# A 128 + 64 channel convolution and a list schedule with measured durations, in layer 0 of a two-layer network

## The chip, the cores and the metric

The kernel runs on one core of one Trainium2 chip. A core has five engines with a queue of instructions each: TensorE (PE, matrix products, with weight loads shown apart as PEld), VectorE (DVE), ScalarE (ACT), GpSimd (POOL) and SyncE (SP, which here only issues DMAs). The metric is the device time of one execution in microseconds (us). Before the change the median of three runs is 8392.63 us (8389.98 to 8398.43).

## The reference

The input x is [2, 96, 96, 96] (images, channels, rows, columns), and everything is float32 unless a step quantizes. Two layers follow each other. Each adds a mixing block to x and then a small feed-forward block (96 to 384 to 96 channels with rounding to 8-bit and 16-bit floats). Layer 0, which the change is about, does this with d_inner = 192 channels, 16 states and four scan directions k:

```
xz = in_proj_w @ layernorm(x);  xin, z = split(xz)          # 192 + 192 channels
t  = gelu(batchnorm(conv3x3(xin, off1_w) + off1_b))          # 192 -> 192 channels
off = tanh(off2_w @ t) / 95                                  # a shift in y and in x
x_s = bilinear sample of xin at (pixel + off)
x_s -> 512 sequences of 36 tokens, by rows and by columns, forward and backward
dt, B, C = x_proj[k] @ x_s;  delta = softplus(dt_proj[k] @ dt + bias)
h[l] = h[l-1] * exp(delta * A) + (delta * x_s) * B[l]        # 16 states per channel
y[l] = sum over states of h[l] * C[l], + D * x_s
out  = out_proj_w @ (layernorm(sum of the 4 directions) * silu(z))
```

Layer 1 is an attention block with a depthwise 5x5 convolution. The change doesn't touch it.

## The kernel before

**Stripes and units.** Layer 0 is cut into 32 stripes of 6 rows by 96 columns (T = 576 tokens, H2 = 288 half of them). A stripe passes three parts. `_l0_front` normalizes, projects, convolves, samples, and stores delta and delta*x_s to DRAM. `_l0_scan` runs the recurrence. `_l0_back` normalizes y, projects it and runs the feed-forward block. The front of stripe n+1 and the back of stripe n-1 are planned between the scans of stripe n.

The scan of a stripe has 64 units: 2 channel halves h, 2 orders o, 2 directions kk, 4 quarters i of the states, 2 halves c of the tokens. `_l0_section` makes the operations of eight units, in this chain:

- spread (L1056, TensorE): the selection matrix `selb` times B into PSUM `bp`, of which there are two
- product (L1060, DVE): `bp` times delta*x_s (`dur`), 128 x 864
- scan (L1076, DVE): the recurrence along 864 elements into `h`, of which there are six
- times C (L1081, GpSimd): `h` times C (`cre`, four buffers)
- states (L1093, TensorE): the products with `fold` that sum over states into `y`
- decay (L1041, ScalarE), once for two units: exp(A * delta) into `dA`

DMAs bring `dlr` and `dur` (two buffers each, L1026) per section and `cre` (L1036) per quarter.

**The convolution** (`convolve`, L567). The 192 channels lie as two halves of 96 partitions. A result of 96 output channels by 288 tokens is the sum of 18 products: 2 input halves by 9 taps. There are 2 output halves and 2 token halves, so 72 products of 96 x 96 weights, each as two passes (records) in float32. Its weights `w_c1` are loaded first of nearly all in `_l0_weights`. The sampled `x_s` and all the operands of the front lie in two halves of 96, too.

**What sets the order.** Every operation of layer 0 is given to a planner (`_Plan`) with an engine, a cost in us, the tiles that it reads and writes, and a due time. `order` simulates the five engines: it always takes the operation that can start first, where a tie within 0.1 us on one engine is decided by the due time. A result reaches another engine after a `LAG` (0.5 to 1.5 us), the same engine after `SAME` (0.06). A tile needs a free buffer before its first operation can start. `issue` emits the instructions in the planned order, and `_in_order` fixes that order on every engine and on SP. At run time an engine that waits for a semaphore holds everything behind it. Costs come from `_cost` (by columns) and, for the chain, from constants in `_l0_section`. Due times spread over a stripe's 64 tau (tau = 3.4): the front of stripe n is due from 64 n - 90 to 64 n - 12 tau, the back from 64 n + 68 to 64 n + 135, a spread 60 tau before its unit.

The pick in `order`, which the change rewrites, is:

```python
key = (max(at, free[e] + 0.1), worth, o.no)
if pick is None or key < pick[0]:
    pick = (key, at, o)
```

Of the kernel before, what the change touches and what calls it, by code (L numbers as in the profile page):

```python
# [90 lines left out]
class _Op:  # L91
    def __init__(self, eng, cost, run, due, tab):
        self.eng, self.cost, self.run, self.due, self.tab = eng, cost, run, due, tab
        self.deps, self.tiles, self.start, self.end = set(), [], None, None
        self.left, self.then, self.ready = 0, [], 0.0

SAME = 0.06  # L100
LAG = {"pe": 0.5, "dve": 1.5, "act": 0.6, "pool": 1.0, "sp": 1.5}


class _Plan:
# [3 lines left out]
    def __init__(self, k):  # L108
        self.k, self.ops, self.slots, self.queues = k, [], {}, {}
        self.rate = {}  # L110
# [12 lines left out]
    def op(self, eng, cost, run, r=(), w=(), due=0.0, tab=None, also=()):  # L123
        o = _Op(eng, cost * self.rate.get(eng, 1.0), run, due, tab)
        ref = lambda t: t if isinstance(t, tuple) else (t, None)
# [20 lines left out]
    def order(self):  # L146
# [13 lines left out]
        while len(out) < len(self.ops):  # L160
            best = None
            for e, queue in ready.items():
                pick = None
                for o in queue:
                    at = max(free[e], o.ready)
                    for t in o.tiles:
                        if t.slot is None:
                            s = t.place()
                            if s is None:
                                at = None  # L170
                                break
                            at = max(at, s[1] + (SAME if s[2] == e else LAG[e]))
# [6 lines left out]
                    key = (max(at, free[e] + 0.1), worth, o.no)  # L179
                    if pick is None or key < pick[0]:  # L180
                        pick = (key, at, o)
# [21 lines left out]
            for p in o.then:  # L203
                p.left -= 1
                p.ready = max(p.ready, o.end + (SAME if p.eng == o.eng else LAG[p.eng]))
# [77 lines left out]
def _l0_weights(k, a, cp, tmp, ps, dram):  # L283
# [6 lines left out]

    k.w_in = load("in_proj", [C, 4 * C])
    k.w_c1 = load("off1", [C, 2, 9, 2 * C])
# [11 lines left out]
    bnv = tmp.tile([C, 5, 2], F32, tag="bnv", name="bnv")  # L304
    nc.sync.dma_start(bnv, a["bn"])
    k.bn_s = cp.tile([C, 2], F32, tag="bn_s", name="bn_s")
    k.bn_t = cp.tile([C, 2], F32, tag="bn_t", name="bn_t")
    nc.scalar.activation(k.bn_s, bnv[:, 4, :], AF.Sqrt, bias=k.eps5[:C])
    nc.vector.reciprocal(k.bn_s, k.bn_s)
    nc.vector.tensor_tensor(k.bn_s, k.bn_s, bnv[:, 1, :], ALU.mult)  # L310
    nc.vector.tensor_tensor(k.bn_t, bnv[:, 0, :], bnv[:, 3, :], ALU.subtract)
    nc.vector.tensor_tensor(k.bn_t, k.bn_t, k.bn_s, ALU.mult)
    nc.vector.tensor_tensor(k.bn_t, k.bn_t, bnv[:, 2, :], ALU.add)


    off2 = tmp.tile([C, 4], F32, tag="off2", name="off2")
    nc.sync.dma_start(off2, a["off2"])
    k.w_off = cp.tile([C, 4, C], F32, tag="w_off", name="w_off")
    nc.vector.tensor_copy(k.w_off, off2.unsqueeze(2).to_broadcast([C, 4, C]))
# [3 lines left out]
    xp = tmp.tile([C, 2, KG, 6 + 2 * NS], F32, tag="xp", name="xp")  # L323
    nc.sync.dma_start(xp, a["x_proj"])
    k.w_dl = cp.tile([C, 2, 2, C], F32, tag="w_dl", name="w_dl")
# [8 lines left out]
    k.w_bc = cp.tile([C, 2, 2, 4, 2, NS], F32, tag="w_bc", name="w_bc")  # L334
# [94 lines left out]
    ds4 = tmp.tile([C, KG, 2], F32, tag="ds4", name="ds4")  # L429
    nc.scalar.dma_start(ds4, a["Ds"])  # L430
    k.Dsum = cp.tile([C, 2], F32, tag="Dsum", name="Dsum")
    nc.vector.tensor_tensor(k.Dsum, ds4[:, 0], ds4[:, 1], ALU.add)
    nc.vector.tensor_tensor(k.Dsum, k.Dsum, ds4[:, 2], ALU.add)
    nc.vector.tensor_tensor(k.Dsum, k.Dsum, ds4[:, 3], ALU.add)
    k.w_D = cp.tile([C, 2, C], F32, tag="w_D", name="w_D")
    for half in range(2):
        nc.vector.tensor_scalar(
            k.w_D[:, half], k.ident[:C, :C], k.Dsum[:, half : half + 1], None, ALU.mult
# [3 lines left out]
def _cost(eng, cols):  # L442

    if eng == "pe":
        return 0.00175 * cols
    if eng == "act":
        return 0.2 + 0.0009 * cols
    if eng == "pool":
        return 0.2 + 0.00177 * cols
    return 0.08 + 0.00115 * cols  # L450


def _op(S):
    def op(eng, n, run, r, w, also=(), tab=None, times=1):
        S.op(eng, times * _cost(eng, n), run, r, w, also=also, tab=tab)
# [4 lines left out]
def _l0_front(k, P, S, f, x, b, s, at):  # L460
# [13 lines left out]
    def pe(cols, run, r, w, also=()):  # L474
        S.op("pe", _cost("pe", cols), run, r, w, also=also)

    def act(cols, run, r, w, tab=None, times=1):
        S.op("act", times * _cost("act", cols), run, r, w, tab=tab)

    def dve(cols, run, r, w):  # L480
        S.op("dve", _cost("dve", cols), run, r, w)

    def pool(cols, run, r, w):
        S.op("pool", _cost("pool", cols), run, r, w)


    xt, xin = temp([C, 8, HW], "xt"), S.tile(P.front, [C, 2, 8, HW + 4], "xin", 1)
# [39 lines left out]
    def project(half, c):  # L527
        pi = ps("pi")
        pe(N4, lambda: nc.tensor.matmul(
            pi.ap[:C, :N4], k.w_in[:, half * C : (half + 1) * C], xn.ap[:, 4 * c : 4 * c + 4, :],  # L530
            start=True, stop=True), ((xn, c),), (pi,), (xin,))
        act(N4, lambda: nc.scalar.copy(
            xin.ap[:, half, 4 * c : 4 * c + 4, 2 : HW + 2],
            pi.ap[:C, :N4].rearrange("p (r w) -> p r w", w=HW)), (pi,), ((xin, (half, c)),))
# [3 lines left out]
    for half in range(2):  # L538
        for c in range(2):
            project(half, c)  # L540

# [18 lines left out]
    t = temp([C, 2, T], "t")  # L560

    def convolve(oh, c):
        pc = ps("pc")

        def part(ih, tap):
            dy, dx = divmod(tap, 3)
            pe(H2, lambda: nc.tensor.matmul(  # L567
                pc.ap[:C, :H2],
                k.w_c1[:, ih, tap, oh * C : (oh + 1) * C],
                xin.ap[:, ih, 3 * c + dy : 3 * c + dy + 3, dx + 1 : dx + 1 + HW],  # L570
                start=(ih == 0 and tap == 0),
                stop=(ih == 1 and tap == 8),
            ), (xin,), (pc,), (t,))

        for ih in range(2):
            for tap in range(9):
                part(ih, tap)
        act(H2, lambda: nc.scalar.activation(
            t.ap[:, oh, c * H2 : (c + 1) * H2], pc.ap[:C, :H2], AF.Gelu,
            bias=k.bn_t[:, oh : oh + 1], scale=k.bn_s[:, oh : oh + 1]),  # L580
            (pc,), ((t, (oh, c)),), tab="g")

    for oh in range(2):
        for c in range(2):
            convolve(oh, c)
# [3 lines left out]
    fr = temp([C, 2, WIN, HW], "fr", 2)  # L589

    def offset(yx, c):
        po = ps("po")

        def run():
            for half in range(2):
                nc.tensor.matmul(
                    po.ap[:C, :H2], k.w_off[:, 2 * half + yx, :],
                    t.ap[:, half, c * H2 : (c + 1) * H2], start=(half == 0), stop=(half == 1))

        pe(2 * H2, run, ((t, (0, c)), (t, (1, c))), (po,), (fr,))  # L600

        def share():
            v = fr.ap[:, yx, 3 * c : 3 * c + 3].rearrange("p r w -> p (r w)")
            nc.scalar.activation(v, po.ap[:C, :H2], AF.Exp, scale=-2.0)
            nc.scalar.activation(v, v, AF.Ln, bias=k.one[:C])
# [8 lines left out]
    xs0 = f.xs0 = S.tile(P.hand, [C, 2, T], "xs0", 2)  # L614
    xs1 = S.tile(P.front, [C, 2, T], "xs1", 1)
    dif, top, bot = temp([C, 2, 7, HW], "dif"), temp([C, 2, WIN, HW], "top", 1), temp([C, 2, WIN, HW], "bot")
# [3 lines left out]
    def sample(half):  # L620
        v = lambda: xin.ap[:, half, 1:8, 2 : HW + 2]
        fy, fx = lambda: fr.ap[:, 0], lambda: fr.ap[:, 1]
# [1344 lines left out]
```

## Time and profile before

| | |
|---|---|
| median of 3 runs | 8392.63 us |
| profiled execution: its time, its span | 8398.9 us, 8397.1 us |
| mean granted TensorE clock | 0.908 |
| DVE busy | 7812.2 us (93%) |
| scan L1076: count, busy, mean | 2048, 3999.5 us, 1954 ns |
| product L1060 | 2048, 2133.7 us, 1043 ns |
| times C L1081 (GpSimd) | 2048, 3497.2 us, 1714 ns |
| decay L1041 (ScalarE) | 3072, 2156.1 us, 765 ns |
| convolution L567 (TensorE): records, busy, mean | 4608, 1334.6 us, 421 ns |
| states L1093 (TensorE) | 18432, 1847.4 us, 448 ns |
| first scan starts, last scan starts | 144.03 us, 6342.84 us |

The profile is of one execution. An engine is busy while an instruction of it runs. Records overlap: two neighbours on DVE by some 0.08 us, matmuls by much more, so a mean is longer than the spacing from start to start. "Idle before" is the time that an engine stood still ahead of an instruction, with the event that ended it. A wait counts only on the engine that sets the pace of its stage. Layer 0 runs until about 6380 us, where layer 1 loads its input, so the page's shares over the whole span mix two layers.

### The profile page before, as it was taken

The page shows a single profiled execution, that of the slowest core. Times are in us where ns is not written, and L with a number is a line of the kernel's source. Part 1 is how long each engine was busy: PE and PEld are TensorE (multiplying, and loading weights), DVE is VectorE, ACT ScalarE, POOL GpSimd, SP SyncE. Part 2 cuts the span into 40 slices and gives each one's busy share as a digit, 9 for nine tenths or more (in the row PEclk, how much of TensorE's full clock was granted, in tenths as well). Part 3 has the DMA queues.
Part 4 walks back from the last instruction along what each step waited for, and adds up shares of the span by engine and source line. Part 5 has one row for each costly group of instructions (what it writes and reads, how often), then busy time and mean ns, then how long its engine had stood idle before and what let it go on. Part 6 is the DMA issues. An engine that isn't in the chain of part 4 may idle for free. (4 is left out here: it accounts for less than half of the span.)

```text
span 8397.1 us, 118884 instructions
## 1 busy us (share of the span) xinstructions
PE 7293.7 (87%) x43653; PEld 3394.8 (40%) x43653; DVE 7812.2 (93%) x5398; ACT 6318.8 (75%) x10674; POOL 5177.2 (62%) x3835
## 2 busy tenths in 40 slices
PE   7888888888888888888888888888857999989998
PEld 4444444444444444444444444444423223542245
DVE  3999999999999999999999999999996998959988
ACT  5778777777777877777777777777745886778867
POOL 4888888788888888878788888888863000110001
PEclk8899998999889999989999889898857999989999
DMA  3444444444444454444444444444441000110001
GB/s 94 152 155 151 155 152 151 151 152 146 152 149 151 157 159 152 151 150 153 149 152 147 151 151 150 157 150 153 152 131 56 3 2 14 37 47 3 2 22 33
DMA packets 339992, 985.62 MB, mean 117 GB/s; under 512 B 50152, under 2 KB 51872, under 8 KB 339104
## 3 DMA queue, kind: packets, MB, share of 16 engines
q1 hardware_dynamic: 337488, 977.74, 37.0%
q8 instruction: 347, 5.69, 0.3%
q14 instruction: 253, 2.07, 0.1%
q10 hardware_dynamic: 1904, 0.12, 0.0%
HBM read 797.19 MB, written 139.25 MB: 112 GB/s over the span
## 5 line engine op out<-in xcount | busy, mean ns | idle before, releaser
L1081 POOL TENSOR_TENSOR h<-h,cre 128x864 f32<-128x864 f32 x2048 | 3497.2, 1714 | 1130.3 <-DVE h L1076 681.5
L1076 DVE TENSOR_TENSOR_SCAN h<-dA,bp 128x864 f32<-128x864 f32 x2048 | 3999.5, 1954 | 96.1 <-PE y L1093 19.1
L1041 ACT ACTIVATE dA<-dlr,A 128x576 f32<-128x576 f32 x3072 | 2156.1, 765 | 767.2 <-DVE h L1076 678.6
L1060 DVE TENSOR_TENSOR bp<-dur,bp 128x864 f32<-128x864 f32 x2048 | 2133.7, 1043 | 93.3 <-DMA dur<-du_d 39.6
L1093 PE MATMUL y<-h,fold 128*32 128x288 f32 (+2 forms) x18432 | 1847.4, 448 | 318.8 <-POOL h L1081 308.0
L567 PE MATMUL pc<-xin,off 96*96 96x288 f32 x4608 | 1334.6, 421 | 0.0
L1093 PEld LDWEIGHTS y<-h,fold 128*32 128x32 f32 x18432 | 761.3, 118 | 1085.4 <-POOL h L1081 579.9
L1056 PE MATMUL bp<-bt,selb 128*128 128x288 bf16 x2048 | 647.5, 317 | 534.1 <-DVE h L1076 512.7
L1429 ACT ACTIVATE pr<-sc 128x960 f32<-128x960 f32 (+1 forms) x1080 | 953.9, 937 | 200.8 <-PE sc L1425 178.6
L1509 DVE TENSOR_TENSOR sums<-sums,pr 128x3840 f32<-128x3840 f32 (+1 forms) x240 | 959.1, 3996 | 56.2 <-ACT pr L1429 34.2
L567 PEld LDWEIGHTS pc<-xin,off 96*96 96x96 f32 x4608 | 721.9, 167 | 410.2 <-issue 156.4
L1601 POOL MEMSET vch<- 96x32 f32 x16 | 2.4, 153 | 1301.7 <-DVE dist L1463 1208.4
L1056 PEld LDWEIGHTS <-selb 128*128 128x128 bf16 x2048 | 200.6, 98 | 1391.3 <-DVE h L1076 1125.1
L1425 PE MATMUL sc<-qH,kH 32*128 32x480 f32 (+1 forms) x3240 | 627.3, 602 | 10.2 <-DMA q<-qH 5.5
L1425 PE MATMUL sc<-q,kH 32*128 32x480 f32 (+1 forms) x1080 | 564.6, 602 | 0.0
L1491 PE MATMUL av<-pr,vT 128*32 128x480 f32 (+1 forms) x4320 | 533.7, 565 | 3.6 <-ACT av L1516 3.5
L1682 DVE SCALAR_TENSOR_TENSOR acc<-vch,lepe_w,acc 96x1152 f32<-96x1152 f32 x320 | 469.2, 1466 | 8.5 <-ACT vch L1617 0.8
L1425 PEld LDWEIGHTS sc<-qH,kH 32*128 32x128 f32 x3240 | 219.1, 184 | 419.8 <-issue 219.4
L883 POOL TENSOR_TENSOR x<-x,fy 96x576 f32<-96x576 f32 x32 | 55.6, 1738 | 478.7 <-ACT fy L882 414.7
L740 PE MATMUL pt<-xd,w_dt 96*128 96x288 f32 x768 | 299.3, 479 | 24.9 <-ACT r L746 11.9
L759 POOL TENSOR_TENSOR e<-e,du 128x576 f32<-128x576 f32 x192 | 231.1, 1204 | 50.5 <-ACT du L755 49.9
L745 ACT ACTIVATE e<-pt,dt_b 128x288 f32<-128x288 f32 x384 | 190.6, 496 | 93.6 <-PE pt L740 89.2
(270 smaller groups left out, 9858.7 us busy)
## 6 DMA issues: line engine op xcount, KB each, us to landing
cre<-c_d SPq DMA_DIRECT2D x1024, 288.0 KB
dur<-du_d SPq DMA_DIRECT2D x256, 864.0 KB
dlr<-dl_d SPq DMA_DIRECT2D x256, 864.0 KB
x<-xs SPq DMA_DIRECT2D x512, 72.0 KB
du_d<-du SPq DMA_DIRECT2D x128, 288.0 KB
dl_d<-dl SPq DMA_DIRECT2D x128, 288.0 KB
du_d<-du SPq DMA_DIRECT2D x128, 144.0 KB
dl_d<-dl SPq DMA_DIRECT2D x128, 144.0 KB
```

The source lines that it names most:

```text
L567: pe(H2, lambda: nc.tensor.matmul(pc.ap[:C, :H2], k.w_c1[:, ih, tap, oh * C : (oh + 1) * C], xin.ap[:, ih, 3 * c + dy : 3 * c + dy + 3, dx ...
L1041: nc.scalar.activation(dA.ap[:, :, blk, :], dlr.ap[:, blk, :].rearrange("p (c n) -> p c n", c=2), AF.Exp, scale=k.A[:, i, kg, h, blk : blk ...
L1056: nc.tensor.matmul(bp.ap[:, :H2], k.selb[:, kk, i, :], f.bc[o].ap[:, toks], start=True, stop=True)
L1060: nc.vector.tensor_tensor(bp.ap[:, : NBL * H2].rearrange("p (b n) -> p b n", b=NBL)[:, ::-1], dur.ap[:, ::-1, toks], bp.ap[:, :H2].unsquee ...
L1076: nc.vector.tensor_tensor_scan(hv, dv, bv, 0.0, ALU.mult, ALU.add)
L1081: nc.gpsimd.tensor_tensor(ht.ap, ht.ap, cre.ap[:, toks].unsqueeze(1).to_broadcast([128, NBL, H2]), ALU.mult)
L1093: nc.tensor.matmul(dst, k.fold, v, start=False, stop=stop)
L1425: nc.tensor.matmul(two[to // 2][:, to % 2, :n], kH[rows, k0 : k0 + 128], q, start=True, stop=True)
L1429: nc.scalar.activation(pr[:, 2 * i : 2 * i + 2, :n], two[i][:, :, :n], AF.Exp, scale=HD**-0.5)
L1491: nc.tensor.matmul((main if s < HEADS else other)[s * HD : (s + 1) * HD, :n], vT[:, blk, hd, :], pr[:, place(s, p), :n], start=at == 0, st ...
L1509: nc.vector.tensor_tensor(both, both, pr[:, :, :, :n], ALU.add)
L1682: S.op("dve", 1.43, lambda: nc.vector.scalar_tensor_tensor(acc.ap, src(), W.lw[:, t : t + 1], acc.ap, ALU.mult, ALU.add), (vch,), (acc,))
```

## The change

Three things change, all in layer 0.

1. The 192 channels lie as 128 + 64 instead of 96 + 96 in `xin`, `t`, `fr`, `x_s` and their weights. A DMA per stripe copies the 64-channel part of `xin` into partitions 64 to 127, shifted by one column, so that one product takes two taps of it. A result then takes 15 products: nine with the 128 channels ("a"), three with 64 channels and two taps, three with 64 channels and the third tap. The first 128 output channels are convolved for each token half; for the other 64, the two token halves go to partitions 0 to 63 and 64 to 127 of one PSUM tile, as pairs of products.
2. The convolution's weights (`w_ca`, `w_cb`) are loaded by five DMAs of the plan instead of one at the start. Small operands (bn, off2, x_proj, Ds) come in two to four DMAs each.
3. The planner has other costs for layer 0 (`fine`), a shorter lag between operations of the chain (`scan=True`), and a rule for a spread (`first=True`): no operation may be placed on TensorE that would end more than `HOLD` after a spread could start. Layer 1 keeps the old costs and has no such operations.

```diff
 SAME = 0.06
 LAG = {"pe": 0.5, "dve": 1.5, "act": 0.6, "pool": 1.0, "sp": 1.5}
+SCAN_LAG = {"pe": 0.2, "dve": 0.3, "act": 0.2, "pool": 0.2, "sp": 1.5}
+HOLD = 0.15
...
-                            at = max(at, s[1] + (SAME if s[2] == e else LAG[e]))
+                            lag = SCAN_LAG if o.scan else LAG
+                            at = max(at, s[1] + (SAME if s[2] == e else lag[e]))
...
-                    key = (max(at, free[e] + 0.1), worth, o.no)
-                    if pick is None or key < pick[0]:
-                        pick = (key, at, o)
+                    cand.append(((max(at, free[e] + 0.1), worth, o.no), at, o))
+                    if o.first:
+                        hold = at + HOLD if hold is None else min(hold, at + HOLD)
+                for c in cand:
+                    if hold is None or c[2].first or c[1] + c[2].cost <= hold:
+                        if pick is None or c[0] < pick[0]:
+                            pick = c
...
-                p.ready = max(p.ready, o.end + (SAME if p.eng == o.eng else LAG[p.eng]))
+                lag = SCAN_LAG if o.scan and p.scan else LAG
+                p.ready = max(p.ready, o.end + (SAME if p.eng == o.eng else lag[p.eng]))
...
+RATE = {"pe": (0.05, 0.00185), "act": (0.08, 0.00107), "pool": (0.14, 0.0018), "dve": (0.03, 0.00108)}
+LOOSE = {"pe": (0.0, 0.00175), "act": (0.2, 0.0009), "pool": (0.2, 0.00177), "dve": (0.08, 0.00115)}
...
+    S.op("sp", 1.0, lambda: nc.sync.dma_start(
+        xin.ap[64:, 1, :, 1 : HW + 1], xin.ap[:64, 1, :, 2 : HW + 2]),
+        ((xin, (1, 0)), (xin, (1, 1))), ((xin, "on"),))
...
+    terms = [("a", dy, dx) for dy in range(3) for dx in range(3)]
+    terms += [("b", dy, None) for dy in range(3)] + [("b", dy, 2) for dy in range(3)]
...
+    def convolve_rest():
+        pc = ps("pc")
+        for n in range(len(terms)):
+            def run(n=n):
+                for c in range(2):
+                    w, v = term(slice(128, 2 * C), c, n)
+                    nc.tensor.matmul(pc.ap[64 * c : 64 * c + 64, :H2], w, v,
+                                     start=n == 0, stop=n == len(terms) - 1)
+
+            S.op("pe", 0.6, run, reads(n), (pc,), also=(t,))
...
-            S.op("act", 0.76, decay, (dlr,), ((dA, blk),), due=t0 - P.early["act"] * tau, tab="e")
+            S.op("act", 0.69, decay, (dlr,), ((dA, blk),), due=t0 - P.early["act"] * tau, tab="e",
+                 scan=True)
...
-        S.op("pe", 0.3, spread, (f.bc[o],), (bp,), due=t0 - P.early["pe"] * tau)
-        S.op("dve", 1.03, product, (dur,), (bp,), due=t0 - P.early["dve"] * tau)
+        S.op("pe", 0.26, spread, (f.bc[o],), (bp,), due=t0 - P.early["pe"] * tau,
+             scan=True, first=True)
+        S.op("dve", 0.96, product, (dur,), (bp,), due=t0 - P.early["dve"] * tau, scan=True)
...
-        S.op("dve", 2.0, scan, (dA, bp), (ht,), due=t0 + (1.35 - P.early["dve"]) * tau)
+        S.op("dve", 1.87, scan, (dA, bp), (ht,), due=t0 + (1.35 - P.early["dve"]) * tau, scan=True)
...
-        S.op("pool", 1.75, times_c, (cre,), (ht,), due=t0 + (2.3 - P.early["pool"]) * tau)
+        S.op("pool", 1.7, times_c, (cre,), (ht,), due=t0 + (2.3 - P.early["pool"]) * tau, scan=True)
...
-        S.op("pe", 1.0, states, (ht,), (py,), due=t0 + (3.5 - P.early["pe"]) * tau)
+        S.op("pe", 0.84, states, (ht,), (py,), due=t0 + (3.5 - P.early["pe"]) * tau, scan=True)
...
-        S, tau = _Plan(k), 3.4
+        S, tau = _Plan(k, True), 3.4
...
+            S.op("sp", 1.0, lambda dst=dst, src=src: nc.sync.dma_start(dst, src), (), (t,),
+                 due=-88 * tau)
```

The five weight loads carry the due time -88 tau, the first stripe's front starts at -90 tau.

## The prediction

> **What bounds the kernel now.** I read the totals first, then the stages, then the waits of the engine that is full, and last the order of instructions around single waits. The page's totals and slices:
>
> ```profile
> PE 7293.7 (87%) x43653; PEld 3394.8 (40%) x43653; DVE 7812.2 (93%) x5398; ACT 6318.8 (75%) x10674; POOL 5177.2 (62%) x3835
> PE   7888888888888888888888888888857999989998
> DVE  3999999999999999999999999999996998959988
> ```
>
> VectorE is full from the second slice to the thirtieth: that is layer 0. Cut by stage (columns: length, busy us of PE, PE weight loads, DVE, ACT, POOL, then granted clock, DMA share, GB/s):
>
> ```profile
> 0.00:144.00 144.00, 106.48 (x352) 61.60 (x353) 17.95 (x97) 72.14 (x136) 43.10 (x56) 0.87 0.27 80
> 400.00:6000.00 5600.00, 4829.98 (x28645) 2355.49 (x28647) 5470.81 (x3872) 4333.87 (x7511) 4561.38 (x3299) 0.91 0.48 151
> 6345.00:8397.00 2052.00, 1926.13 (x11979) 780.98 (x11976) 1739.93 (x1023) 1540.60 (x2401) 128.71 (x174) 0.95 0.08 21
> ```
>
> So there are three parts: 144 us until the first scan, some 6201 us of scanning, 2052 us of tail and layer 1, which the change doesn't touch. In the middle DVE is busy 5471 of 5600 us, so only idle time can be won there. How much is the floor? An undisturbed stretch of the timeline:
>
> ```profile
> 3002.99 1.04 DVE L1060 TENSOR_TENSOR bp<-dur,bp 128x864 f32<-128x864 f32 x1
> 3004.07 1.95 DVE L1076 TENSOR_TENSOR_SCAN h<-dA,bp 128x864 f32<-128x864 f32 x1
> 3005.94 1.04 DVE L1060 TENSOR_TENSOR bp<-dur,bp 128x864 f32<-128x864 f32 x1
> ```
>
> One unit (product, scan) takes 3005.94 - 3002.99 = 2.95 us. Over two units it is 2.945 (the product after next starts at 3008.88), so 2048 units are about 6031 us; six other DVE instructions a stripe (two each of L928, L524, L843: 0.73, 0.53, 0.43 us less 0.08 of overlap) add 32 x 2.9 = 93. From 144.0 to the end of the last scan at 6344.8 are 6200.8, so some 77 us are idle. The waits of DVE from 144 to 6345 say for whom (total us, times, longest):
>
> ```profile
> DVE bp L1060 <- PE bp L1056: 38.6, 39, 3.3
> DVE h L1076 <- PE y L1093: 19.1, 14, 2.2
> DVE bp L1060 <- POOL h L1081: 9.2, 7, 1.9
> DVE h L1076 <- ACT dA L1041: 5.7, 1, 5.7
> DVE bp L1060 <- PE y L1093: 3.7, 4, 1.7
> ```
>
> With four smaller ones they sum to 80.2. TensorE ends 38.6 + 19.1 + 3.7 = 61.4 of it, though it is not full. Why, one such place of the timeline shows:
>
> ```profile
> 2309.95 2.13 PE L908 MATMUL yva<-ysq,mean 96*96 96x288 f32 x4
> 2312.00 1.18 PE L1093 MATMUL y<-h,fold 128*32 128x288 f32 x6
> 2313.30 1.95 DVE L1076 TENSOR_TENSOR_SCAN h<-dA,bp 128x864 f32<-128x864 f32 x1 [2.20 <-PE y L1093]
> ```
>
> Four `both` operations of the back part run in a row, the fold of h (L1093) that frees the scan's buffer stands behind them, and the scan starts 2.20 us late. Ahead of the scans, the convolution of the first stripe:
>
> ```profile
> 36.48 35.22 PE L567 MATMUL pc<-xin,off 96*96 96x288 f32 x144
> ```
>
> Here nothing hides it: ScalarE, GpSimd and DVE wait, and everything up to the first scan follows in series.
>
> **What the Trainium skill says.** "TensorE: Matmul & The Clock Gate", Part 3, What overlaps: matmuls keep strict order, only weight loads move ahead. The stall above agrees: the fold isn't drawn past 2.13 us of others. "TensorEngine Tiling (Array Packing)", Tiling Modes: 128 x 64 column tiles are two, and different tiles run in parallel; the trace has it for 32-column tiles (three L1093 products of 288 columns take 0.69 us at 3003.85), not for 64. "DMA: Bandwidth & Descriptors", Anatomy of one DMA: about 2 us are fixed; the trace's xt load, issued at 18.09, was used at 23.04, so it does not contradict it.
>
> **The change, part by part.**
>
> *Convolution.* Before: 4 results of 18 products, 72 products in two passes each (144 records), 35.22 / 72 = 0.489 us. After: 15 products per result (nine of 128 input channels, three of 2 x 64 stacked by the shifted copy, three of 64), for two results of 128 output channels, and 15 pairs for the other 64 channels. Rounds: 15 + 15 + 15 = 45, 22.0 us, if the halves of a pair run beside each other; 60, 29.3 us, if not. By the L1093 row I take 45. In the first stripe that saves 13.2 us (bounds 5.9 and 13.2) on the path to the first scan. In the later ones TensorE gets 13.2 of some 194 us back, worth nothing directly, since DVE is the bound; it only thins the blocks. One Gelu fewer (0.59 us) on ScalarE, 77% busy, is hidden by the scans; if ScalarE were the bound it would be 19 us in all.
>
> *Shifted copy.* One more DMA a stripe on SP, 64 x 8 rows of 384 B, 197 KB against 151 GB/s x 194 us = 29 MB. Issue 0.5 us (as other SP rows), landing some 2 us. Behind it on SP stand the loads of cre, dlr, dur. Four cre buffers at 5.9 us a quarter give them about 3 x 5.9 = 17.7 us of lead, so a short wait costs nothing. On TensorE, the nine products that don't need it (4.4 us) hide its landing. I take 0; without that cover 2 us, paid once in the first stripe. The later stripes have slack.
>
> *Setup.* The 1296 KB of weights leave the first load (issued at 1.21; SP's next issue was at 9.89) and come as five DMAs in the plan, most of them before xt. Eleven more small DMAs (bn, off2, xp, Ds in parts) at 0.3 to 0.5 us are about +4.5 us on SP; some have 4-byte runs, and no row shows those. Against it stands a gap of 8.3 us in SP's issues that goes. xt then lands behind about 1 MB, which took 6 to 8 us at the start. I take 0, bounds -6 and +6.
>
> *Operands.* Projection, sampling, x_dbl and D products keep their counts and free sizes; only partitions change. 0.
>
> *The planner.* This is the largest term and no row prices it. The old costs give a unit 1.03 + 2.0 + 0.06 = 3.09 us against 2.945 measured: the plan thinks DVE slower than it is, and puts up to 0.15 us too much between two scans. The new one gives 0.96 + 1.87 + 0.06 = 2.89, now a little short: other engines wait for DVE rather than the reverse. With `first`, nothing may stand on TensorE that would end over 0.15 us after a spread could start; so four pairs in a row can't stand before a waiting spread. Bounds: all 61.4 us of PE waits go; or the order is no better and 0 goes; below that, new waits (a rival). TensorE has room: from a unit of 2.945 the plan takes 0.26 + 0.84 for spread and fold, which leaves 1.85 x 64 = 118 us a stripe for the rest, about 80 at the new costs (convolution 45 x 0.58 = 26, 22 pairs of products at 1.12 = 25, two groups of five at 2.7, single products the rest). I take three quarters, 46 us, since waits for late operands at the head of TensorE's queue remain. Of the 18.8 us of other waits I take 5 (a shorter lag puts times-C and fold nearer to the scan); bounds 0 and 19.
>
> *Sum on the profiled execution* (8398.9 us; span 8397.1 and 1.8 around it): 8398.9 - 13 - 46 - 5 = 8335. The median of the runs, 8392.63, lies 6.3 below the profiled one: **8329 us**, -0.76%. What is late next is DVE itself: 2.945 us a unit.
>
> **Rivals.** *A, only the start is won:* the blocks are replaced by others, TensorE still ends most waits. For it: 39 + 14 waits in 2048 units are rare events, which any new order throws anew; against it: the hold addresses just these. Time 8393 - 13 = 8380 (to 8376 with a few us of waits).
>
> *B, slower: SP's head blocks.* SP issues in order; if the shifted copy stands before its ScalarE copies are done by more than the lead of cre (17.7 us less some 4 to land, so from about 14 us), scans wait for cre through h, 32 times. At 17 us: 3 x 32 = 96, less the 64 won: 8425. For it: SP did sit at xt from 18.83 to 75.67 in the first stripe. Against: the plan knows when the projection ends, the x_s stores wait likewise today, and SP's longest wait for POOL in the middle is 8 us.
>
> *C, better:* every listed wait goes and the setup gains 6: 8393 - 13 - 80 - 6 = 8294.
>
> *D, the pairs don't run side by side:* 8329 + 7 = 8336; inside the forecast, as it only moves the start.
>
> **How the numbers follow.** A measurement here tells about 0.2%, 17 us, from nothing: below 8376 is faster, above 8409 slower. The forecast with D (8300 to 8366): 0.65. C: 0.08. A: 0.14, of which 0.03 lies below 8376. B, or waits for POOL or ACT of that size from the tighter lags: 0.13. Faster 0.65 + 0.08 + 0.03 = 0.76, same 0.11, slower 0.13. The range from 8296 to 8388 holds the forecast, nearly all of A and half of C. It leaves out B and a little of C, under 2 in 10.
>
> **What would show it.** The first scan near 131 instead of 144. The convolution near 22 us in the first stripe, 90 records plus 30 that overlap. DVE's waits for spreads below 10 us and for folds below 8. A unit still 2.945. A stripe of 6200.8 / 32 = 193.8 us falling to about 192.2. If instead DVE waits stand at POOL's h or at dA, the lags are too short for the real engines; if they stand at dur or cre landings, it is B; if the first scan stays at 144, front(1) filled the room or the weights came late.

## The result and the profile after

| | before | after |
|---|---|---|
| median of 20 runs each | 8397.77 us (8389.98 to 8415.25) | 8364.95 us (8346.97 to 8400.17) |
| ratio, 95% interval | | 0.9962 (0.9954 to 0.9969) |
| profiled execution: its time, its span | 8398.9, 8397.1 us | 8360.85, 8359.0 us |
| first scan starts | 144.03 us | 146.78 us |
| first scan to the end of the last ("scan phase") | 6200.8 us | 6159.8 us |
| the rest, layer 1 above all | 2052.3 us | 2052.4 us |

The kernel is 0.38% faster, some 33 us of the 64 that the prediction gave (8392.63 to 8329). The start became 2.8 us longer, the scan phase 41 shorter. The totals and the DVE slices of the page after hardly differ:

```profile
PE 7186.7 (86%) x42885; PEld 3103.1 (37%) x42885; DVE 7626.3 (91%) x5404; ACT 6253.0 (75%) x10610; POOL 5183.8 (62%) x3835
...
DVE  3999999999999999999999999999996998959988
```

DVE is busy 186 us less (7812.2 before) for the same 4096 products and scans. The windows of the kernel after (length, busy us of PE, weight loads, DVE, ACT, POOL, clock, DMA share, GB/s) place that in the middle:

```profile
0.00:147.00 147.00, 113.54 (x335) 57.84 (x336) 18.81 (x104) 72.87 (x136) 43.14 (x56) 0.83 0.29 84
400.00:6000.00 5600.00, 4737.60 (x28056) 2091.56 (x28052) 5318.74 (x3885) 4280.79 (x7465) 4577.24 (x3302) 0.89 0.48 153
6307.00:8359.00 2052.00, 1928.66 (x11982) 781.41 (x11976) 1740.14 (x1023) 1540.72 (x2401) 127.66 (x174) 0.95 0.08 21
```

In the same 5600 us DVE ran 3885 instructions after and 3872 before, in 5319 us of busy time against 5471. So an instruction costs DVE less, and DVE stands still more. Both were unforeseen.

**Why a unit is cheaper.** An undisturbed stretch of DVE's timeline after (start, duration; x2 is two in a row):

```profile
3001.68 2.00 DVE L1112 TENSOR_TENSOR bp<-dur,bp 128x864 f32<-128x864 f32 x2
3003.59 3.79 DVE L1129 TENSOR_TENSOR_SCAN h<-dA,bp 128x864 f32<-128x864 f32 x2
3007.30 2.00 DVE L1112 TENSOR_TENSOR bp<-dur,bp 128x864 f32<-128x864 f32 x2
3009.21 3.79 DVE L1129 TENSOR_TENSOR_SCAN h<-dA,bp 128x864 f32<-128x864 f32 x2
```

DVE no longer alternates. It runs product, product, scan, scan: two units from 3001.68 to 3007.30 are 5.62 us, 2.81 a unit against 2.945 before. All steps from start to start on DVE in the two traces, medians in us (count):

| step | before | after |
|---|---|---|
| product to scan | 1.075 (2015) | 0.961 (1011) |
| product to product | | 0.949 (985) |
| scan to scan | | 1.864 (968) |
| scan to product | 1.871 (1884) | 1.844 (946) |

Before, each scan follows the product that it reads, and starts 1.075 us after it. After, another product or scan stands between, and the step is 0.95 to 0.96. A pair costs 0.949 + 0.961 + 1.864 + 1.844 = 5.618, so 2.809 a unit: 0.136 us less, some 278 us over 2048 units. This is worked out from the medians, as if every unit stood in a pair; 985 of the 1024 possible pairs do. The mean durations hide it, because the records of neighbours overlap: 1936 + 1046 ns after against 1954 + 1043.

**Where it went.** The groups of the page after show the idle time ahead of scan and product (last column, with what ended most of it):

```profile
L1129 DVE TENSOR_TENSOR_SCAN h<-dA,bp 128x864 f32<-128x864 f32 x2048 | 3888.1, 1936 | 145.1 <-PE y L1146 136.1 <-ACT dA L1092 7.1 <-POOL h L1134 1.2
L1112 DVE TENSOR_TENSOR bp<-dur,bp 128x864 f32<-128x864 f32 x2048 | 2063.7, 1046 | 200.5 <-PE bp L1108 65.2 <-DMA dur<-du_d 46.2 <-PE y L1146 43.3
```

In the scan phase the waits of DVE for TensorE are 136.1 + 65.2 + 43.3 = 244.6 us, against 61.4 before. Phase less units less the 93 us of other DVE instructions leaves 6160 - 5753 - 93 = 314 us idle, against 77. So 278 us were won and 237 given back, which is the 41.

The largest single item is unit 38 of the stripe: 103 us in the 31 stripes after the first, as 24 waits in 16 stripes, nearly every second one. Nearly all of it falls where `direct`, described below, stands behind the 40th spread of its stripe in TensorE's order; where it stands ahead of the 39th, DVE waits there at most 0.7 us. So this stall is one of the planned order. One such place in the timeline of all engines:

```profile
2380.73 1.28 ACT L576 ACT_TABLE_LOAD   x1
2382.49 2.24 PE L573 MATMUL pz<-xn,in_proj 96*96 96x288 f32 x4 [2.77 <-ACT zs L576]
2382.62 0.57 ACT L1043 COPY Y<-y 96x504 f32<-96x504 f32 x1
2384.66 1.05 PE L1033 MATMUL y<-xs,w_D 128*32 128x504 f32 x1
2387.80 1.54 PE L1146 MATMUL y<-h,fold 128*32 128x288 f32 x24
2388.54 3.80 DVE L1129 TENSOR_TENSOR_SCAN h<-dA,bp 128x864 f32<-128x864 f32 x2 [8.69 <-PE y L1146]
```

At unit 32 the channel half changes. `y` must be copied out (L1043) and refilled (L1033, `direct`) before the folds of the new half can run. Here both come late, behind the next front's gate on ScalarE (L576, with a table load) and on TensorE (L573). Six units fit into the six `h` buffers, then the scan waits 8.69 us for the folds.

### The profile page after: what moved, and what is told of

Its sections match the earlier page's. It is cut to its first block, busy times and chain, and to the rows that moved or that the text cites. A ratio compares the mean times of both kernels' runs of the same rounds, so it can differ in the third digit from the quotient of the medians.

```text
span 8359.0 us, 117497 instructions
## 1 busy us (share of the span) xinstructions
PE 7186.7 (86%) x42885; PEld 3103.1 (37%) x42885; DVE 7626.3 (91%) x5404; ACT 6253.0 (75%) x10610; POOL 5183.8 (62%) x3835
## 5 line engine op out<-in xcount | busy, mean ns | idle before, releaser
L1129 DVE TENSOR_TENSOR_SCAN h<-dA,bp 128x864 f32<-128x864 f32 x2048 | 3888.1, 1936 | 145.1 <-PE y L1146 136.1
L1112 DVE TENSOR_TENSOR bp<-dur,bp 128x864 f32<-128x864 f32 x2048 | 2063.7, 1046 | 200.5 <-PE bp L1108 65.2
L1146 PE MATMUL y<-h,fold 128*32 128x288 f32 (+2 forms) x18432 | 1824.8, 449 | 87.6 <-POOL h L1134 81.9
L611 PE MATMUL pc<-xin,w_ca 128*128 128x288 f32 x1152 | 370.1, 425 | 0.0
L791 PE MATMUL pt<-xd,w_dt 96*128 96x288 f32 x768 | 319.1, 508 | 10.2 <-ACT r L797 4.9
L812 POOL TENSOR_TENSOR dl<-dl,r 128x576 f32<-128x576 f32 x192 | 231.0, 1203 | 26.4 <-ACT dl L809 16.1
L611 PE MATMUL pc<-xin,w_cb 128*128 128x288 f32 (+1 forms) x768 | 244.5, 429 | 0.0
```

What stands on the lines that cost most here:

```text
L611: nc.tensor.matmul(pc.ap[:, :H2], w, v, start=n == 0, stop=n == len(terms) - 1)
L1112: nc.vector.tensor_tensor(bp.ap[:, : NBL * H2].rearrange("p (b n) -> p b n", b=NBL)[:, ::-1], dur.ap[:, ::-1, toks], bp.ap[:, :H2].unsquee ...
L1129: nc.vector.tensor_tensor_scan(hv, dv, bv, 0.0, ALU.mult, ALU.add)
L1146: nc.tensor.matmul(dst, k.fold, v, start=False, stop=stop)
```

## The experiments

All twelve beside the two kernels. "Steps" counts product directly followed by a scan, some 2000 if they alternate and 1000 in pairs. "Waits" is DVE's idle time in gaps over 0.1 us, in the 31 stripes after the first. The kernel before took 8402 to 8410 us beside them.

| run | median us | ratio (95%) | scan phase | steps | waits | clock |
|---|---|---|---|---|---|---|
| before | | 1 | 6200.8 | 2015 | 73 | 0.908 |
| after | 8364.95 | 0.9962 (0.9954 to 0.9969) | 6159.8 | 1011 | 284 | 0.897 |
| e1 new convolution, old planner | 8465.73 | 1.008 (1.0063 to 1.0097) | 6258.3 | 1967 | 117 | 0.867 |
| e2 old convolution, new planner | 8604.76 | 1.0245 (1.0228 to 1.0262) | 6398.3 | 1025 | 510 | 0.911 |
| e3 after, no pairs | 8400.06 | 0.9995 (0.9986 to 1.0004) | 6203.9 | 2002 | 83 | 0.885 |
| e4 after, no hold | 8238.14 | 0.9807 (0.9791 to 0.9824) | 6038.8 | 1217 | 117 | 0.910 |
| e5 neither | 8352.26 | 0.9942 (0.9925 to 0.9959) | 6157.7 | 2003 | 34 | 0.898 |
| e6 = e2, no hold | 8517.03 | 1.0137 (1.012 to 1.0154) | 6310.8 | 1219 | 367 | 0.915 |
| e7 = e1 + useless products | 8464.36 | 1.007 (1.0053 to 1.0086) | 6266.1 | 2012 | 128 | 0.900 |
| e8 after, HOLD 0.9 | 8234.00 | 0.9808 (0.9782 to 0.9834) | 6028.6 | 1180 | 115 | 0.916 |
| e9 = e8, old lag | 8518.17 | 1.0135 (1.0118 to 1.0152) | 6314.0 | 1988 | 169 | 0.886 |
| e10 after, y due early | 8473.13 | 1.008 (1.0063 to 1.0097) | 6272.6 | 1020 | 379 | 0.886 |
| e11 after, front 1 late | 8396.57 (1 run) | | 6198.7 | 1014 | 323 | 0.895 |
| e12 before, front 1 late | 8407.40 (1 run) | | 6203.6 | 2011 | 81 | 0.905 |

**The two halves of the change apart.** e1 is the kernel after with the old lag, costs and no hold; e2 is the kernel before with the new ones.

```diff
 # e1, against after
-                            lag = SCAN_LAG if o.scan else LAG
+                            lag = LAG
...
-             scan=True, first=True)
+             scan=True)
-        S, tau = _Plan(k, True), 3.4
+        S, tau = _Plan(k), 3.4
...
 # e2, against before: lag, costs and hold as in the change, the convolution stays
+                            lag = SCAN_LAG if o.scan else LAG
...
-        S.op("pe", 0.3, spread, (f.bc[o],), (bp,), due=t0 - P.early["pe"] * tau)
+        S.op("pe", 0.26, spread, (f.bc[o],), (bp,), due=t0 - P.early["pe"] * tau,
+             scan=True, first=True)
```

> The convolution, the 128 + 64 layout and the weight loads of the changed kernel, with the old planner (old costs, LAG everywhere, no first). Theory 1 (the changed kernel's gain comes from DVE issuing two products and then two scans, which the shorter lag brings about): no pairs here, a unit is 2.945 us again, DVE's waits in the scan phase stay between 60 and 100 us, the first scan starts at 140 to 148 us; 8380 to 8400 us. Theory 2 (the gain comes from the thinner work on TensorE): 8355 to 8375 us.

> The old convolution and layout with the new planner (costs, SCAN_LAG, first and HOLD). Theory 1: pairs of products and scans as in the changed kernel (about 1000 product-to-scan steps instead of 2015), so the floor of a unit falls to 2.81 us, but long waits at a few places of a stripe take it back and more, since 13 us more of convolution a stripe have to pass the hold: 8400 to 8600 us. Theory 2: 8385 to 8400 us, the gain is gone with the convolution.

Each half alone makes the kernel slower, by 0.8 and 2.45%; together they make it faster. Neither theory gave the time of e1, and e2 lies 5 us above the first one's range. The wait of DVE in e1 that grew most (total us, times, longest; 38.6 before):

```profile
DVE bp L1112 <- PE bp L1108: 120.4, 179, 3.2
```

and in e2 (19.1 before):

```profile
DVE h L1089 <- PE y L1106: 341.1, 85, 13.1
```

In e2 the pairs are there (1025 steps), but the folds come late: 267 us of its 510 lie at unit 6. So the convolution alone is not the thing that gains. That it makes room for the new order, e6 tests below.

**Pairs and hold.** e3 lets the scan be due before the next product (0.9 tau instead of 1.35), e4 takes the hold away, e5 does both.

```diff
 # e3, against after
-        S.op("dve", 1.87, scan, (dA, bp), (ht,), due=t0 + (1.35 - P.early["dve"]) * tau, scan=True)
+        S.op("dve", 1.87, scan, (dA, bp), (ht,), due=t0 + (0.9 - P.early["dve"]) * tau, scan=True)
 # e4, against after
         S.op("pe", 0.26, spread, (f.bc[o],), (bp,), due=t0 - P.early["pe"] * tau,
-             scan=True, first=True)
+             scan=True)
```

> The changed kernel with one number changed: a scan is due 0.9 tau after its unit's start instead of 1.35, so that it goes ahead of the next unit's product. Theory 1: product and scan alternate, a unit is 2.945 us, and because a spread has a whole unit of time again the waits fall to 20 to 60 us: 8335 to 8380 us, so pairing wins and loses about the same. Rival (the waits of the changed kernel don't come from pairing but from the hold and the tight lags): the waits stay near 300 us on the higher floor, 8500 us or more.

> The changed kernel without first, so that no room is kept on TensorE for spreads. Theory 3 (the hold makes TensorE wait for its spreads and so makes the long waits at the change of the channel half, unit 38): these waits (some 110 us) go, the pairs mostly stay, 8230 to 8330 us. Theory 4 (the hold does what it is there for): waits for spreads rise from 65 us to over 150 us, 8365 to 8480 us.

> The changed kernel with both edits: no first, and a scan due at 0.9 tau. If pairing is what made the kernel without the hold fast (theory 1), a unit is 2.945 us again and this one loses 0.137 us for each of some 800 pairs of steps against it: 8340 to 8390 us, with 30 to 90 us of DVE waits in the scan phase. If instead the missing hold alone did it, some 8240 to 8300 us.

Without pairs the kernel after is the kernel before again (0.9995), 20 us above the range expected, with waits of 83 us instead of 20 to 60. Its largest waits for TensorE:

```profile
DVE bp L1112 <- PE bp L1108: 42.4, 37, 2.6
DVE h L1129 <- PE y L1146: 20.7, 12, 4.3
```

Before it was 38.6 and 19.1. So with the hold, the convolution, the costs and the lags together took nothing off the waits that the prediction wanted to cut by three quarters. Without it they did: e5 alternates like the kernel before, and its waits for TensorE are

```profile
DVE bp L1112 <- PE bp L1108: 31.5, 34, 3.3
DVE h L1129 <- PE y L1146: 0.5, 1, 0.5
```

That is 32 us against 61.4 before. Its scan phase is 43 us shorter than the one before (6157.7 against 6200.8), near the 51 that the prediction gave, but without the rule to which it gave them. The scan phases give the size of each part: pairs are worth 6203.9 - 6159.8 = 44 us with the hold and 6157.7 - 6038.8 = 119 without. The hold costs 121 us with pairs (e4 to after) and 46 without (e5 to e3). In e4 DVE waits 0.7 us for folds in all; its largest wait for TensorE is

```profile
DVE bp L1112 <- PE bp L1108: 95.9, 98, 3.4
```

so in pairs a rule made to keep TensorE clear for spreads did cut the waits for spreads (95.9 to 65.2), and paid for it with 136.1 + 43.3 us of waits for folds, which it holds back like everything else. In the alternating order it did not even cut those for spreads: 31.5 us in e5, 42.4 in e3.

**The old convolution in the new order.** e6 is e2 without the hold.

```diff
 # e6, against e2
-             scan=True, first=True)
+             scan=True)
```

> The old convolution and layout with the new costs and SCAN_LAG, without first. Theory 5 (the convolution's saving of 13 us of TensorE a stripe is what the paired order needs, since folds and the products of D must pass between its products): DVE waits for folds of 200 us or more stay at units 6 and 38, 8400 to 8620 us. Rival (the convolution is worth nothing to the scan): the waits fall as in the kernel without the hold, 8240 to 8320 us.

```profile
DVE h L1089 <- PE y L1106: 269.8, 77, 7.1
```

This is the fold wait of e6, 224 us of all its waits at unit 6 and 43 at unit 38. Removing the hold helps here too (6398.3 to 6310.8), but with the long convolution the scan phase is 272 us longer than in e4. The two differ in all of the convolution's half: the products, the layout and the weight loads. In e6 `direct` stands behind a run of convolution products in the planned order. One place shows it, at a full granted clock: from 2531.22 us twenty records of the convolution run for 5.03 us, `direct` starts at 2538.01, the folds at 2538.88, and the scan at 2539.60, 7.12 us late.

**Why the new convolution alone is slower.** In e1 the granted clock is 0.85 over 400 to 6000 us, against 0.91 before. (Its records are either 1.0 or 0.5, called half clock below.) e7 puts useless work back: the first product of each convolution group runs ten times.

```diff
 # e7, against e1
+            for again in range(9 if n == 0 else 0):
+                pe(H2, lambda: nc.tensor.matmul(
+                    pc.ap[:, :H2], *term(slice(0, 128), c, 0), start=True, stop=True),
+                    reads(0), (pc,), (t,))
 # likewise for the pairs of the other 64 channels
```

> The kernel with the convolution alone, and with useless work put back: the first product of each group of the convolution is issued ten times (each starts the sum anew, so the result is the same), 27 rounds of 0.49 us, 13 us a stripe, so that TensorE has again what the old convolution had. Theory 6 (the short convolution alone was slower because TensorE, with less to do, falls to half its clock, and the spreads and folds take longer then): the granted clock in the scan phase rises from 0.85 to 0.89 or more, waits for spreads fall from 120 us to under 80, and the kernel is faster for having more work: 8390 to 8445 us. Rival (the order or the extra DMA made it slow): 8466 us or more, since TensorE is fuller.

The window of 400 to 6000 us in e1:

```profile
400.00:6000.00 5600.00, 4785.63 (x27721) 2159.34 (x27719) 5426.13 (x3833) 4203.71 (x7355) 4509.12 (x3265) 0.85 0.48 151
```

and in e7, with its waits:

```profile
400.00:6000.00 5600.00, 5014.13 (x29746) 2302.77 (x29741) 5425.58 (x3837) 4213.35 (x7371) 4529.61 (x3273) 0.90 0.49 151
```

```profile
DVE bp L1123 <- PE bp L1119: 64.6, 54, 2.5
DVE h L1140 <- PE y L1157: 30.8, 18, 3.7
```

The clock came back to 0.90 and the waits for spreads fell from 120.4 to 64.6, but waits elsewhere came in their place (128 us in all against 117, those for folds 46.8 against 1.3), and the total stayed (8464 against 8466), outside both ranges. So the clock can account for spread waits of e1, but not for its time. The waits of e1 are 44 us longer than before, of 57 in the scan phase; what brings them is not settled, and with the added products the plan is another one as well.

**How much hold.** 

```diff
 # e8, against after
-HOLD = 0.15
+HOLD = 0.9
```

> The changed kernel with HOLD = 0.9 instead of 0.15, about the time that a pair leaves its second spread. If a late spread costs only beyond that slack: waits of 38 units' boundary stay away as without the hold and waits for spreads fall from 96 us: 8200 to 8240 us. If any hold delays the folds: 8260 to 8365 us.

A hold of 0.9 us does what no hold does (8234.0 and 8238.1). This is 1.9% faster than the kernel before, and 1.6% faster than the kernel after: the version that beats both. Its waits for folds are 2.7 + 0.8 us (ahead of products and of scans), against 43.3 + 136.1 after.

**What brings the pairs.** In the plan a product may start when its spread is done, which itself waits for the buffer of `bp` that the scan two units back frees. With the new lags that takes 0.2 + 0.26 + 0.3 = 0.76 us after that scan, less than the 0.96 of the product running then; with the old ones 0.5 + 0.3 + 1.5 = 2.3. So the next product counts as ready when the running one ends, and is due before the scan (1 tau against 1.35). e9 is e8 with the old lag.

```diff
 # e9, against e8
-SCAN_LAG = {"pe": 0.2, "dve": 0.3, "act": 0.2, "pool": 0.2, "sp": 1.5}
+SCAN_LAG = LAG
```

> The kernel after with HOLD 0.9 as in e8, and SCAN_LAG set equal to the old LAG, all else as after. Theory 1 (the short lag between operations of the chain is what lets the planner think a product ready while the one before it runs, and so brings the pairs): product and scan alternate again (over 1900 steps product to scan instead of e8's 1180), the step product to scan is 1.07 us again, a unit's floor 2.945, waits on DVE under 80 us, scan phase 6150 to 6230, time 8330 to 8420 against e8's 8234. Rival (the pairs come from the measured durations, 0.96 and 1.87, and the due times alone): 1000 to 1300 steps product to scan, scan phase near e8's 6029, time 8220 to 8260.

The lag alone turns the pairs off: 1988 steps, product to scan back at 1.075 us. The rival falls. The time lies 98 us above the range, because the waits for spreads came to

```profile
DVE bp L1112 <- PE bp L1108: 174.4, 138, 3.4
```

where under 80 in all was expected. They lie at units 10 to 15. In the 5 us up to the end of a wait TensorE was at half clock for 97% of the time, weighted by the length of the waits. The same figure is 73% before, 92% in e5, 66% after, and only 30 and 24% in e2 and e6, where the order alone makes DVE wait; of 400 to 6000 us, 17 to 29% are at half clock. Whether the clock makes the waits or falls with them, no run tells apart. e5 and e9 both alternate, with no hold and one of 0.9 us; that the short lag cut the waits from 169 to 34 us is likely, but the due time of the scan differs as well.

**Can the stall at unit 38 be lifted?** e10 makes the two operations around `y` due 60 tau earlier, like spread and fold.

```diff
 # e10, against after
-        S.op("pe", 1.4, direct, (f.xs0,), (py,), due=t0)
+        S.op("pe", 1.4, direct, (f.xs0,), (py,), due=t0 - P.early["pe"] * tau)
...
-        S.op("act", 1.4, out, (py,), (f.Y,), due=t0 + 33 * tau)
+        S.op("act", 1.4, out, (py,), (f.Y,), due=t0 + (33 - P.early["act"]) * tau)
```

> The kernel after with the same HOLD, but the operations that free and refill y between the two channel halves (out on ScalarE, direct on TensorE) due 60 tau earlier, as the spread, fold and decay of the same unit are. Theory 3a (the stall of 103 us at unit 38 comes from these two being due after work of the next stripe's front, which the hold then drags out): the waits at unit 38 fall from 103 to under 60 us in 31 stripes, scan phase 6080 to 6125, time 8285 to 8335. Rival (it comes from the hold alone, whatever is due): the waits at unit 38 stay at 90 to 110, or move to other units in the same sum of some 280 us, time 8350 to 8380.

Unit 38 fell from 103 to 57.5 us as the first theory has it, 12 waits in 7 stripes instead of 24 in 16, but the sum of the waits rose from 284 to 379. Units 27, 11 and 33 now take 38.8, 37.7 and 31.5. The first theory missed the time by 138 us, the rival by 93. The due times set where the stall lies; with the hold in place its time is not lifted but lands elsewhere.

**The start.** The convolution of stripe 0 is 11.0 us shorter (35.22 to 24.2), yet the first scan comes 2.8 later. e11 and e12 keep stripe 1's front out of stripe 0's, in the kernel after and before.

```diff
 # e11, e12
-        (),
+        P.late,
         (xt,),
...
+                P.late = (F[0].du[0], F[0].du[2]) if n == 1 else ()
```

> The kernel after, with the load of stripe 1's x planned only after stripe 0's du is written (its front is then planned behind stripe 0's front, no operation of it between). Theory S1 (the 11 us that the shorter convolution wins at the start are eaten because stripe 1's front is interleaved with stripe 0's): the convolution ends by 60, the first scan starts between 131 and 139 instead of 146.8. Rival S2 (stripe 0's own chain after the convolution is longer or slower for another reason, such as TensorE at half clock): the first scan stays between 142 and 149, with the 82 us from the end of the convolution to it kept within 4 us. No forecast for the whole time but that the scan phase stays within 1.5% of 6160.

> The kernel before with the same edit: stripe 1's front planned behind stripe 0's. Under S1 the interleaving costs the kernel before little (it has 72 us from the end of the convolution to the first scan, against 82 after): the first scan stays between 139 and 144, so that the convolution's gain, 7 to 12 us, shows between this run and the other. Under S2 both runs keep their first scans within 3 us of 144.0 and 146.8.

The first scan is at 143.98 in e11 and 148.60 in e12 (one execution each). S1 falls: keeping stripe 1's front out wins the kernel after only 2.8 us, and costs the kernel before 4.6, more than S2 allows for it. Convolution to scan is 81.4 us in e11 (82.8 after), as S2 has it. Where the 11.0 us went, the lead of the kernel after over the kernel before shows, taken at the same instruction in both timelines (us):

| | before | after | lead |
|---|---|---|---|
| first convolution product | 36.48 | 39.81 | -3.3 |
| last Gelu of the convolution | 71.74 | 64.04 | 7.7 |
| last copy of `x_s` (to `xs1`) | 93.55 | 87.30 | 6.3 |
| first copy of `xd` | 96.67 | 93.85 | 2.8 |
| first store of `du` | 111.36 | 110.03 | 1.3 |
| first load of `dur` | 130.97 | 132.28 | -1.3 |
| first scan | 144.03 | 146.78 | -2.8 |

Two of these losses are TensorE running slower. The x_dbl products of stripe 0 in the kernel after:

```profile
91.55 2.27 PE L751 MATMUL pd<-xs,w_dl 128*96 128x288 f32 x4
93.74 1.43 PE L726 MATMUL pb<-xs,w_bc 128*128 128x288 f32 x4
95.10 1.38 PE L751 MATMUL pd<-xs,w_dl 128*96 128x288 f32 x4
96.41 1.43 PE L726 MATMUL pb<-xs,w_bc 128*128 128x288 f32 x4
```

and in e11:

```profile
85.53 2.48 PE L751 MATMUL pd<-xs,w_dl 128*96 128x288 f32 x4
87.94 2.58 PE L726 MATMUL pb<-xs,w_bc 128*128 128x288 f32 x4
90.45 2.48 PE L751 MATMUL pd<-xs,w_dl 128*96 128x288 f32 x4
92.86 2.58 PE L726 MATMUL pb<-xs,w_bc 128*128 128x288 f32 x4
```

The same sixteen records take 4.1 us before (95.43 to 99.48), 4.8 in e12, 6.2 after and 9.85 in e11. The granted clock over 84 to 104 us is 0.84 before, 0.66 in e12, 0.67 after, 0.50 in e11. The clock is not all of it. From 93.5 to 100.3 us the kernel after has full clock, and its groups of four records still follow at 1.34 us (93.74 to 97.77), where before they follow at 1.00 (96.47 to 99.48, full clock as well). In the whole traces, at full clock, the records of these products follow at 0.32 to 0.35 us (medians) with 128 and 64 rows in turn, and at 0.24 with 96 and 96. So some 1.3 of the 2.1 us come with the new layout. With nothing of stripe 1 between, e11 leads e12 by 10.5 us at the first copy of `x_s` (76.40 against 86.87) and by 3.9 at the first Abs behind these products (98.96 against 102.82). The other piece is ahead of the convolution: the eight `pi` records of the kernel after take 6.17 us against 3.85, and eight of `pz` 4.16 against 3.05. The first is not the change's alone: in e12, with the old layout, the eight `pi` records take 5.43. For the second, e11 has the same 4.16 at a granted clock of 0.50; in the kernel after, the clock has no record before 42.27 us, so half clock there is likely and not shown. The last 4.1 us, from the `du` store to the scan, are not settled: the clock is 0.65 against 0.73 there, and e11 wins back 2.8. All these are single executions, and the start varies: in e3, e4, e5, e8 and e10, with the same convolution, the first scan starts between 142.9 and 147.3 us.

## Why the prediction was right and wrong

**The direction and the range held, the size did not.** On the profiled execution 64 us were forecast and 38 came (8398.9 to 8360.85). Of the 26 missing, 16 are the start (-13 forecast, +2.8 measured), 10 the scan phase (-51 forecast, -41 measured). The second figure looks close, but it is a difference of two terms, -278 and +237, of which the prediction had neither.

**"A unit still 2.945", and DVE itself as what is late next: wrong.** The floor was taken from the order of the kernel before; in pairs a unit takes 2.809, from the medians of its steps. 2.945 is a property of that order: the step from a product to the scan that reads it has 0.114 us that another instruction between them hides. The diff had what was needed to see it, a lag under which the next product is ready before the running one ends and a scan due later than it; I looked at the lag only as a distance between engines. "VectorE: DVE Perf Modes", The DRAIN you can't avoid, of the Trainium skill says that between chained copies a semaphore costs nothing extra. That does not carry over to this case: a scan behind a product that it doesn't read starts after 0.961 us, behind its own after 1.075. Whether the semaphore or the operand makes the difference, no run tells apart.

**"I take three quarters, 46 us", the planner's term: wrong.** e3 has the new convolution, costs, lags and hold without pairs, and gains nothing (waits 83 against 73). With pairs the waits for TensorE were 244.6 us instead of the 15 forecast. The failing step is "TensorE has room", a mean over the stripe of 118 us free for 80 of work. Waits come from what stands in the queue at a given moment, and in pairs the second spread has about one product, 0.95 us, of slack where it had most of a unit. The hold was argued only from what it keeps away from spreads. The prediction's own list named the folds (19.1 us) as waits of TensorE, but it did not ask what the hold does to them. With the hold they rise from 0.7 us (e4) to 179 (after), and the scan phase by 121. In the alternating order that the prediction had in mind, e5 reaches the size of its term without the hold (scan phase 43 us shorter), and the hold takes it back (46 us, e5 to e3). Rival A's sentence that the blocks are replaced by others is right for this term.

The place that the prediction showed as such a block also has a second reading that it did not give. Before, the granted clock is 0.50 from 2303 to 2313.3 us, and the four records of L908 at 2309.95 take 2.13 us, where four of L676 with as many columns take 1.13 at full clock (96.47). So about half of that block's length goes with the half clock, not with the order alone.

**"On the path to the first scan", 13.2 us: half right.** 45 rounds and pairs side by side were right (forecast 22.0 us, measured 24.2), and rival D fell: 36 records of 64 columns took 4.61 us where 18 of 128 columns took 4.65 (L624 at 56.32, L611 at 48.62). But the time was put on the path whole, with all else on TensorE at its old speed. The sixteen records ahead of it and the sixteen behind the sampling took about half as long again. Their durations show some 5.5 of the lost us (3.4 and 2.1). Of the 2.1, some 1.3 come with the layout; of the rest, what lowers the clock is not settled (in e7, with its longer convolution, it is 0.50 over 84 to 104 us as well).

**"It only thins the blocks", the later convolutions worth nothing directly: wrong.** In the new order and without the hold the shorter convolution, with its layout and weight loads, is worth 6310.8 - 6038.8 = 272 us (e6 against e4); with the old planner it costs 57 (e1).

**"Operands ... only partitions change. 0": wrong for TensorE.** Where an operation takes a product of 128 rows and one of 64, its records follow more slowly at full clock: x_dbl at 0.32 to 0.35 us against 0.24, the offsets (`po`) at 0.34 to 0.35 against 0.24. The D products (`direct`) of the second channel half take 2.00 us against 1.06, those of the first half 1.06 as before. By these medians 48 records and one `direct` cost some 5 us a stripe more (an estimate), of the 13.2 that the convolution was to give back.

**Right at zero:** the shifted copy and the setup. The copy landed 3.1 us after its issue in the median, not 2; in the first stripe this was ahead of the convolution's first product. No wait for `cre` appears among DVE's waits, so rival B did not occur; waits for GpSimd's `h` and for `dA` grew, but only from 9.2 and 5.7 to 15.1 and 15.6 us.

## What to carry to other kernels

Before a floor is called a floor, see which order of instructions it was measured in: put an independent instruction between a producer and its consumer on the same engine, and measure from start to start, since mean durations hide the difference. A rule that keeps an engine clear for one kind of work also holds back what frees that work's buffers, so price the release of buffers with it (here `HOLD` at 0.9 instead of 0.15 turns a gain of 0.4% into one of 1.9%). A step shortened in a serial start pays only if the steps around it keep their speed.

## What the runs showed of the hardware

- On DVE a scan after the product that it reads starts 1.075 us behind it, one after another product 0.961; a product after a scan 1.871 in the alternating order, 1.844 in pairs.
- Two products of 64 output columns, to the two halves of one PSUM tile, run beside each other: 18 such pairs took from 56.32 to 60.76 us, 0.247 a pair of records, against 0.249 for a record of 128 columns (18 from 48.62 to 53.11).
- At full clock, f32 records of 288 columns follow at 0.24 us in the old layout's products of 96 and 96 rows, and in a run of convolution products of 128 rows; where products of 128 and 64 rows take turns, at 0.32 to 0.35 us (L726, L751, L645 and L646).
- In these traces the records of the granted clock have only two values, 0.5 and 1.0, so the mean of a window gives the share of half clock: over 400 to 6000 us 18% before (0.91), 22% after, 29% in e1, 20% in e7. Less convolution work went with more time at half clock in e1, but not in e4 and e8, which have the same convolution in pairs (18 and 17%). The records begin 27 to 43 us into the span, so a mean over the start is no measurement there. "TensorE: Matmul & The Clock Gate", Part 1, has these two states and lets the full one follow some 3.4 us of busy time. e11 does not agree: TensorE's records fill 19.6 of the 20 us from 84 to 104, and the granted clock is 0.50 there and over 104 to 147. The durations go with it: sixteen records take 9.85 us, against 4.1 in the kernel before.
